# A graph layer on Trainium2: two small operands of VectorE's wide instructions moved from SBUF to PSUM

## The chip, the core and the metric

The kernel runs on one core of a Trainium2 chip. The time is the device time of one execution in microseconds (us), the median of three timed executions. Beside these there is one more execution, recorded by the profiler, from which every duration in this document comes. Five engines matter: PE (matrix products), DVE (VectorE), ACT (ScalarE), POOL (GpSimd, which here issues the gathers) and SP (which issues the plain transfers). SBUF and PSUM are the two memories on the core.

## The reference

One layer of graph attention over 12,500 nodes of 128 features and 200,000 edges, which come sorted by their target node.

```
h      = relu(layernorm(x))
score  = (h[dst] W_Q^T . h[src] W_K^T) / sqrt(128) * exp(-edge_weight)
keep   = the 16 best scores of each target node
alpha  = softmax of the kept scores, per target node
agg    = sum over kept edges of alpha * (h[src] W_msg^T)
out    = x + relu(h W_self^T + agg)
```

## The kernel before, in words

A short head computes `h` for all nodes, writes it to a table in DRAM (`h_tab`), and lays the edge data out in SBUF so that each partition holds one edge of a chunk of 128. After that the kernel is one long unrolled loop over G = 112 windows of GC = 14 chunks (1,792 edges). A window also looks at the first chunk of the next one, so up to NJ = 15 chunks take part. Nearly everything below has a width of 15 x 40 = 600 elements per partition: 15 chunks by KM = 40 slots (or WN = 40 node columns).

The rows `h[src]` come by indirect gathers on POOL (`gather`, L399): one instruction fetches 128 rows of 512 bytes by a column of 128 row numbers that lies in SBUF (`ix`, or `idx_all` for the first two windows). A window needs 14 gathers, so the whole kernel has 1,563. They go out in pairs: `let_go` (L414) copies two columns of row numbers on DVE and then issues two gathers; `hs` has seven buffers.

The steps of one window, on the other engines:

- `places` (L477, L479; DVE) makes two masks. `ow` compares the numbers 0..39 (`slots`, a 128 x 40 constant in SBUF, made once at L149) with each edge's node column (`dlw`); `po` compares the same numbers with each edge's place among the edges of its node (`pos_all`). Both are 600 elements wide.
- `q_to_edges` (L490; PE) brings the query rows to the edges; `scores` (L500; DVE) multiplies them with the gathered rows, one instruction for a chunk.
- `scores_in_slots` (L508; DVE, 600 wide), `slots_by_node` (L515; PE), `slots_out` (L520; ACT), `best` (L529 to L541; DVE), `sum_of_exps` (L546; ACT) find the 16 best scores of each node and their sum of exponentials.
- `kept_to_edges` (L558; PE) and `on_edges` (L564 to L571; DVE) carry the result back to the edges. L569 multiplies the PSUM tile `px` (named x in the trace) with `po`, 600 wide. `exps` (L575; ACT) takes exponentials.
- `weights` (L579, L580; DVE) multiplies them into `kept`, a factor for each edge, and spreads the factors over `ow` into `alz`, 600 wide.
- `sums` (L590; PE) multiplies `alz` with the gathered rows into a PSUM bank (`bank("a", 1)`, taken anew for each window, one buffer), `sums_out` (L595; ACT) reads it, and L598 to L616 finish and store the window's output.

The order on each engine is the order of the calls in the loop at L630 to L676, because scheduling is manual. One pass `i` works on several windows at once: `weights(i-3)` comes before `places(i+1)`, then `best(i-2)`, `scores(i)` in four parts, and `sums(i-3)` in two parts; `sums_out(i-3)` comes near the end. The waits between engines are put in by the compiler from the tiles that instructions touch. The trace shows that it keeps two instructions apart that touch different columns of the same PSUM bank: L598 writes columns 256 to 383 of the bank `s`, and its weight load starts at 1004.74 us in one window, after L610, which reads columns 384 to 511 of it, has ended at 1004.62; the same holds in the other windows.

A general path for other inputs (L679 on) is skipped at run time.

Of the kernel before, what the change touches and what calls it, by code (L numbers as in the profile page):

```python
# [15 lines left out]
OP = mybir.AluOpType  # L16
# [4 lines left out]
P = 128  # L21
# [10 lines left out]
NJ = GC + 1  # L32

KM = 40

WN = 40
# [22 lines left out]
def bc(ap, n):  # L59

    return ap.unsqueeze(2).to_broadcast([ap.shape[0], ap.shape[1], n])
# [7 lines left out]
def bm(ap, n):  # L69

    return ap.unsqueeze(1).to_broadcast([ap.shape[0], n, ap.shape[1]])
# [3 lines left out]
def gnn_layer(  # L75
# [27 lines left out]
    nc = tc.nc  # L103
# [26 lines left out]
    def bank(tag, bufs):  # L130
        return psum.tile([P, 512], F32, tag=tag, bufs=bufs, name=tag)
# [16 lines left out]
    slots = const.tile([P, KM], F32, name="slots")  # L148
# [12 lines left out]
    dlw = const.tile([P, G, NJ], F32, name="dlw")  # L161
# [224 lines left out]
    with tc.tile_pool(name="win", bufs=2) as win, tc.manual_schedule():  # L386
        chunks = [min(NJ, CH - GC * g) for g in range(G)]
        own = [min(GC, CH - GC * g) for g in range(G)]

        T = [{} for _ in range(G)]  # L390

        so = bank("s", 1)
        et = bank("e", 1)

        def gather(g, j0, j1, index):
            if j0 == 0:
                T[g]["hs"] = rows_pool.tile([P, GC, D], F32, name="hs", bufs=7)
            for j in range(j0, j1):
                nc.gpsimd.indirect_dma_start(  # L399
                    out=T[g]["hs"][:, j, :], out_offset=None, in_=h_tab[0:N, :],  # L400
                    in_offset=bass.IndirectOffsetOnAxis(ap=index(j), axis=0))

        def rows_of(g, j):
            return T[g]["hs"][:, j, :] if j < GC else T[g + 1]["hs"][:, 0, :]

        def let_go(g, k):

            j0, j1 = 2 * k, min(2 * k + 2, own[g])
            if j0 >= j1:
                return  # L410
            if k == 0:
                T[g]["ix"] = win.tile([P, GC], I32, name="ix", bufs=4)
            ix = T[g]["ix"]
            nc.vector.tensor_copy(ix[:, j0:j1], idx_all[:, GC * g + j0:GC * g + j1])  # L414
            gather(g, j0, j1, lambda j: ix[:, j:j + 1])
# [58 lines left out]
        def places(g):  # L474
            n = chunks[g]
            T[g]["ow"] = win.tile([P, NJ, WN], F32, name="ow", bufs=6)
            nc.vector.tensor_tensor(T[g]["ow"][:, 0:n, :], bm(slots, n), bc(dlw[:, g, 0:n], WN), op=OP.is_equal)  # L477
            T[g]["po"] = win.tile([P, NJ, KM], F32, name="po", bufs=5)
            nc.vector.tensor_tensor(T[g]["po"][:, 0:n, :], bm(slots, n),  # L479
                                    bc(pos_all[:, GC * g:GC * g + n], KM), op=OP.is_equal)  # L480


# [92 lines left out]
            nc.scalar.activation(T[g]["up"][:, 0:n], T[g]["up"][:, 0:n], AF.Exp)  # L575

        def weights(g):
            n, kept = chunks[g], T[g]["kept"]
            nc.vector.tensor_tensor(kept[:, 0:n], T[g]["up"][:, 0:n], kept[:, 0:n], op=OP.mult)  # L579
            nc.vector.tensor_tensor(alz[g % 2].rearrange("e (j w) -> e j w", w=WW + STEP)[:, 0:n, 0:WN],  # L580
                                    T[g]["ow"][:, 0:n, :], bc(kept[:, 0:n], WN), op=OP.mult)


        def sums(g, part):
            n = chunks[g]
            if part == 0:
                T[g]["pa"] = bank("a", 1)
            half = n // 2
            for j in range(half) if part == 0 else range(half, n):
                nc.tensor.matmul(T[g]["pa"][:, 0:P], lhsT=alz[g % 2][:, WW * j + PRE:WW * j + PRE + P],  # L590
                                 rhs=rows_of(g, j), start=(j == 0), stop=(j == n - 1))
# [35 lines left out]
        for g in range(min(2, G)):  # L627
            gather(g, 0, own[g], lambda j: idx_all[:, GC * g + j:GC * g + j + 1])

        for i in range(-3, G + 6):  # L630
# [5 lines left out]
            at(i - 5, output)  # L636
            at(i - 5, store)
            at(i - 3, weights)
            more(0)
            at(i - 4, sums_turned)  # L640
# [3 lines left out]
            at(i + 1, far_of)  # L644
            at(i - 1, slots_by_node)
            at(i + 1, places)
            more(1)
            at(i - 2, best)
# [8 lines left out]
            at(i + 1, q_parts)  # L657
            at(i + 2, h_turned_out)
            at(i - 3, sums, 0)
            at(i - 2, kept_to_edges)  # L660
            at(i, scores, 1)
            more(4)
            at(i, q_to_edges, 3)
            at(i - 2, one_over_sum)
            at(i - 3, sums, 1)
            at(i, scores, 2)
            at(i - 2, on_edges)
# [190 lines left out]
```

## Time and profile before

| | us |
|---|---|
| three timed executions | 2797.12, 2806.0, 2806.96; median 2806.0 |
| the profiled execution | 2125.5 |
| its span, first to last instruction | 2123.7 |
| POOL busy in the span | 1544.1 (73%) |
| DVE busy | 1488.2 (70%) |
| PE busy | 1312.0 (62%) |
| ACT busy | 626.7 (30%) |

The timed executions are 680 us longer than the profiled one. The profile doesn't show what the difference is made of. In the profiled execution the first gather starts at 79.9 us and the last at 2084.5 us, so nearly the whole span is the loop; a window takes about 17.9 us. A row of the profile names the line, the engine, the operation and the tiles (out<-in); "busy, mean ns" is the group's total and the mean of one, and what stands behind the bar is the idle time of the engine just before these instructions, with what ended it. A row of the timeline has the start in us, the duration in us and the instruction; a bracket gives the idle time before it.

### The profile page before, as it was taken

How to read it: one execution, taken by the hardware profiler on the slowest of the kernel's cores; microseconds unless marked ns; L12 is line 12 of the kernel's file. 1: busy time of each engine (PE TensorE's matmuls, PEld its weight loads, DVE VectorE, ACT ScalarE, POOL GpSimd, SP SyncE). 2: the span in 40 equal slices, each digit the busy share in tenths (PEclk: the TensorE clock that was granted, in tenths of full speed). 3: DMA queues.
4: the chain of work that ended last, by engine and by line, in shares of the span. 5: the costliest groups of instructions: out<-in, count | busy, mean ns of one | idle time of the engine just before them, and what ended most of it. 6: DMA issues, size and time to landing. Idle time of an engine off the chain costs nothing. (4 is left out here: it accounts for less than half of the span.)

```text
span 2123.7 us, 43559 instructions
## 1 busy us (share of the span) xinstructions
PE 1312.0 (62%) x14574; PEld 1210.1 (57%) x14575; DVE 1488.2 (70%) x7474; ACT 626.7 (30%) x1225; POOL 1544.1 (73%) x1585
## 2 busy tenths in 40 slices
PE   1166666666666666666666666666666666666665
PEld 1155566555555655555555656565666666565654
DVE  7667677777776777767777767677777776777764
ACT  3442222222222222222222222222222222222220
POOL 1477777777777777777777777777777777777773
PEclk9977877877777877877777777777777787877787
DMA  8453343333343343333333334334433343333420
GB/s 220 146 162 116 119 120 119 120 119 119 120 119 119 116 122 115 115 112 119 118 119 119 119 119 120 119 119 120 120 119 120 119 120 120 119 119 119 120 67 24
DMA packets 118805, 253.18 MB, mean 119 GB/s; under 512 B 33030, under 2 KB 76297, under 8 KB 118558
## 3 DMA queue, kind: packets, MB, share of 16 engines
q1 hardware_dynamic: 67336, 144.92, 19.7%
q0 software_dynamic: 50144, 102.74, 19.1%
q10 hardware_dynamic: 1094, 2.69, 0.5%
q8 instruction: 115, 1.88, 0.4%
q14 instruction: 116, 0.95, 0.1%
HBM read 236.40 MB, written 14.40 MB: 118 GB/s over the span
## 5 line engine op out<-in xcount | busy, mean ns | idle before, releaser
L399 POOL DMA_INDIRECT hs<-h_tab,ix x1535 | 1495.9, 975 | 467.8 <-issue 335.9
L500 DVE SCALAR_TENSOR_TENSOR prod<-hs,dec_all,q 128x128 f32<-128x128 f32 x1674 | 516.9, 345 | 334.3 <-DMA hs<-h_tab,ix 319.1
L490 PE MATMUL q<-q,to_e 128*128 128x128 bf16 x5022 | 464.2, 254 | 33.1 <-DVE prod L500 32.3
L598 PE MATMUL s<-ident,agn 128*128 128x128 f32 x112 | 49.3, 440 | 662.2 <-DVE kept L579 661.7
L490 PEld LDWEIGHTS <-to_e 128*128 128x128 bf16 x5022 | 410.1, 116 | 56.0 <-issue 39.8
L590 PE MATMUL a<-hs,alz 128*128 128x128 f32 x3348 | 425.8, 281 | 0.8 <-DVE alz L580 0.8
L598 PEld LDWEIGHTS s<-ident,agn 128*128 128x128 f32 x112 | 20.2, 180 | 678.4 <-issue 676.7
L590 PEld LDWEIGHTS a<-hs,alz 128*128 128x128 f32 x3348 | 404.4, 197 | 1.2 <-DVE alz L580 1.1
L515 PE MATMUL e<-ow,sl 128*41 128x40 f32 x3348 | 251.3, 265 | 8.4 <-DVE sl L508 8.4
L515 PEld LDWEIGHTS e<-ow,sl 128*41 128x41 f32 x3348 | 235.7, 184 | 23.6 <-DVE sl L508 9.2
L466 ACT ACTIVATE far<-dstb,nb 128x1920 bf16<-128x1920 int32 x112 | 212.9, 1901 | 5.1 <-DMA dstb<-in_dst_dram 5.1
L471 ACT ACTIVATE to_e<-far 128x1920 bf16<-128x1920 bf16 x112 | 201.2, 1796 | 0.1
L602 ACT COPY aggT<-s 128x128 f32<-128x128 f32 x112 | 29.8, 266 | 507.8 <-PE s L598 507.8
L529 DVE TENSOR_SCALAR ell<-slots,e 128x40 f32<-128x40 f32 x112 | 28.3, 253 | 205.3 <-PE e L515 192.6
L546 ACT ACTIVATE e<-v,km 128x16 f32<-128x16 f32 x112 | 34.4, 308 | 363.5 <-DVE km L538 363.5
L500 DVE DVE_READ_ACCUMULATOR prod<-hs,dec_all,q 128x1 f32 x1674 | 139.1, 83 | 0.2
L414 DVE COPY ix<-idx_all 128x2 int32<-128x2 int32 (+1 forms) x768 | 132.7, 173 | 0.0
L575 ACT ACTIVATE up<-up 128x15 f32<-128x15 f32 x112 | 24.1, 215 | 336.5 <-DVE up L567 336.4
L595 ACT ACTIVATE agn<-a,rden 128x128 f32<-128x128 f32 x112 | 41.2, 368 | 209.8 <-PE a L590 209.8
L508 DVE TENSOR_TENSOR sl<-po,s 128x600 f32<-128x600 f32 x112 | 87.5, 781 | 3.9
L580 DVE TENSOR_TENSOR alz<-ow,kept 128x600 f32<-128x600 f32 x112 | 87.5, 781 | 3.8
L399 POOL DMA_INDIRECT hs<-h_tab,idx_all x28 | 33.7, 1203 | 77.6 <-DMA x_end<-zpad 69.4
(150 smaller groups left out, 1562.7 us busy)
## 6 DMA issues: line engine op xcount, KB each, us to landing
dstb<-in_dst_dram SPq DMA_DIRECT2D x111, 960.0 KB
hs<-h_tab,ix POOLq DMA_INDIRECT x1535
h_r<-h_tab SPq DMA_DIRECT2D x112, 64.0 KB
x_t<-in_x_dram SPq DMA_DIRECT2D x108, 64.0 KB
out_dram<-o SPq DMA_DIRECT2D x108, 64.0 KB
xg<-in_x_dram SPq DMA_DIRECT2D x10, 560.0 KB
h_tab<-xg SPq DMA_DIRECT2D x10, 560.0 KB
dst_r<-in_dst_dram ACTq DMA_DIRECT2D x1, 803.2 KB
```

Source lines behind the costliest of these rows:

```text
L399: nc.gpsimd.indirect_dma_start(out=T[g]["hs"][:, j, :], out_offset=None, in_=h_tab[0:N, :], in_offset=bass.IndirectOffsetOnAxis(ap=index(j ...
L414: nc.vector.tensor_copy(ix[:, j0:j1], idx_all[:, GC * g + j0:GC * g + j1])
L466: nc.scalar.activation(T[g]["far"][:, 0:n], T[g]["dstb"][:, 0:n], AF.Square, bias=nb[:, g:g + 1])
L471: nc.scalar.activation(T[g]["to_e"][:, 0:n], T[g]["far"][:, 0:n], AF.Relu, bias=1.0, scale=-1.0)
L490: nc.tensor.matmul(pq[:, (j - j0) * P:(j - j0 + 1) * P], lhsT=T[g]["to_e"][:, j * P:(j + 1) * P], rhs=upper(T[g]["q"][:, k, :]), start=(k ...
L500: nc.vector.scalar_tensor_tensor(prod, rows_of(g, j), dec_all[:, c:c + 1], T[g]["pq", b][:, (j % 4) * P:(j % 4 + 1) * P], op0=OP.mult, op1 ...
L508: nc.vector.tensor_tensor(sl1[g % 2][:, 0:n, 0:KM], T[g]["po"][:, 0:n, :], bc(T[g]["s"][:, 0:n], KM), op=OP.mult)
L515: nc.tensor.matmul(et[0:KM + 1, STEP * j:STEP * j + WN], lhsT=sl1[g % 2][:, j, :], rhs=T[g]["ow"][:, j, :], start=False, stop=(j == n - 1))
L580: nc.vector.tensor_tensor(alz[g % 2].rearrange("e (j w) -> e j w", w=WW + STEP)[:, 0:n, 0:WN], T[g]["ow"][:, 0:n, :], bc(kept[:, 0:n], WN) ...
L590: nc.tensor.matmul(T[g]["pa"][:, 0:P], lhsT=alz[g % 2][:, WW * j + PRE:WW * j + PRE + P], rhs=rows_of(g, j), start=(j == 0), stop=(j == n ...
L595: nc.scalar.activation(T[g]["agn"], T[g]["pa"][:, 0:P], AF.Copy, scale=T[g]["rden"])
L598: nc.tensor.transpose(so[:, 2 * P:3 * P], T[g]["agn"], ident)
```

## The change

A PSUM bank `ab` is taken once for the loop. The slot numbers are copied into its columns 256 to 295 once; `places` reads them from there. `weights` writes its factors into the columns 384 to 398 of the same bank and reads them from there. `sums` writes its result into columns 0 to 127 of it, in place of a bank taken anew for each window. The work and its order on every engine are otherwise the same. There are no added instructions inside the loop; there is one added copy before it.

```diff
         so = bank("s", 1)
         et = bank("e", 1)
 
+        ab = bank("a", 1)
+        nc.vector.tensor_copy(ab[:, 2 * P:2 * P + KM], slots)
+
...
-            nc.vector.tensor_tensor(T[g]["ow"][:, 0:n, :], bm(slots, n), bc(dlw[:, g, 0:n], WN), op=OP.is_equal)
+            nc.vector.tensor_tensor(T[g]["ow"][:, 0:n, :], bm(ab[:, 2 * P:2 * P + KM], n), bc(dlw[:, g, 0:n], WN), op=OP.is_equal)
             T[g]["po"] = win.tile([P, NJ, KM], F32, name="po", bufs=5)
-            nc.vector.tensor_tensor(T[g]["po"][:, 0:n, :], bm(slots, n),
+            nc.vector.tensor_tensor(T[g]["po"][:, 0:n, :], bm(ab[:, 2 * P:2 * P + KM], n),
                                     bc(pos_all[:, GC * g:GC * g + n], KM), op=OP.is_equal)
...
         def weights(g):
-            n, kept = chunks[g], T[g]["kept"]
-            nc.vector.tensor_tensor(kept[:, 0:n], T[g]["up"][:, 0:n], kept[:, 0:n], op=OP.mult)
+            n, kept = chunks[g], ab[:, 3 * P:3 * P + NJ]
+            nc.vector.tensor_tensor(kept[:, 0:n], T[g]["up"][:, 0:n], T[g]["kept"][:, 0:n], op=OP.mult)
             nc.vector.tensor_tensor(alz[g % 2].rearrange("e (j w) -> e j w", w=WW + STEP)[:, 0:n, 0:WN],
                                     T[g]["ow"][:, 0:n, :], bc(kept[:, 0:n], WN), op=OP.mult)
...
         def sums(g, part):
             n = chunks[g]
-            if part == 0:
-                T[g]["pa"] = bank("a", 1)
+            T[g]["pa"] = ab
```

## The prediction

> **What bounds the kernel now.** First the page's busy times and its costliest groups:
>
> ```profile
> PE 1312.0 (62%) x14574; PEld 1210.1 (57%) x14575; DVE 1488.2 (70%) x7474; ACT 626.7 (30%) x1225; POOL 1544.1 (73%) x1585
> ...
> L399 POOL DMA_INDIRECT hs<-h_tab,ix x1535 | 1495.9, 975 | 467.8 <-issue 335.9
> L500 DVE SCALAR_TENSOR_TENSOR prod<-hs,dec_all,q 128x128 f32<-128x128 f32 x1674 | 516.9, 345 | 334.3 <-DMA hs<-h_tab,ix 319.1
> ```
>
> No engine is at 100%, so busy shares don't name the bound; the idle times do. POOL's 467.8 us before 1535 gathers is 0.305 us each. The view of POOL's waits (total us, times, longest us) shows that this is a constant, whatever ended it:
>
> ```profile
> POOL hs L399 <- issue: 343.8, 1128, 0.3
> ...
> POOL hs L399 <- DVE prod L500: 34.4, 113, 0.3
> POOL hs L399 <- DMA hs<-h_tab,ix: 31.1, 102, 0.3
> POOL hs L399 <- DVE ix L414: 26.8, 88, 0.3
> ```
>
> The view of line L399 gives the gathers' shortest, median and longest duration in ns:
>
> ```profile
> L399 POOL DMA_INDIRECT hs<-h_tab,ix x1535: 940/944/1550, 122.1 to 2084.5; - x192
> ```
>
> The longest wait of every kind is 0.3 us: in the loop POOL never waits for data or a buffer. (Its row numbers are copied about 30 us ahead, as the trace's L414 starts show.) A gather's median is 944 ns, so POOL's beat is 0.944 + 0.305 = 1.249 us, and 14 of them make 17.49 us against a window of 17.9 us. DVE in turn waits for gathered rows (319 us, some 2.9 us a window), so it follows POOL. The loop is bound by POOL's chain of gathers; a microsecond counts only if it shortens that chain.
>
> The chain has a defect: the mean is 975 ns where the median is 944 and the maximum 1550. 1535 x (975 - 944) = 47.6 us, 46.9 when I add up the excess gather by gather. The timeline shows where it is:
>
> ```profile
> 1004.32 0.94 POOL L399 DMA_INDIRECT hs<-h_tab,ix  x1 [0.30 <-issue]
> ...
> 1004.74 0.78 DVE L580 TENSOR_TENSOR alz<-ow,kept 128x600 f32<-128x600 f32 x1
> ...
> 1005.51 0.78 DVE L477 TENSOR_TENSOR ow<-slots,dlw 128x600 f32<-128x600 f32 x1
> 1005.56 1.54 POOL L399 DMA_INDIRECT hs<-h_tab,ix  x1 [0.30 <-issue]
> ...
> 1006.20 0.78 DVE L479 TENSOR_TENSOR po<-slots,pos_all 128x600 f32<-128x600 f32 x1
> ...
> 1007.41 0.94 POOL L399 DMA_INDIRECT hs<-h_tab,ix  x1 [0.30 <-issue]
> ...
> 1018.21 0.77 DVE L569 TENSOR_TENSOR mine<-x,po 128x600 f32<-128x600 f32 x1
> ...
> 1018.64 0.94 POOL L399 DMA_INDIRECT hs<-h_tab,ix  x1 [0.30 <-issue]
> ```
>
> The gather of 1005.56 starts under L477, both of whose inputs are in SBUF, and takes 1.54 us. The gather of 1018.64 starts under L569, which is as wide but reads one input from PSUM (x), and takes 0.94. Over the whole loop, put down to the instruction that ran when the gather started: L477 39.1 us, L479 5.5, L508 2.5, L460 0.3, all others nothing. Of the gathers that overlap L569 the mean is 943 ns.
>
> **The change part by part.**
>
> *L477 and L479 read the slot numbers from PSUM.* They keep one SBUF input, as L569 has now. By the L569 row their stalls go: 39.1 + 5.5 = 44.6 us. [...] What is late next: the freed gathers start the next beat 0.4 us a window earlier, DVE's waits for rows shrink from 2.9 us to about 2.5 a window, and POOL stays the bound.
>
> *L580 reads its factors from PSUM.* No gather loses time under it now (0 us): it ends just before a gather starts. So 0 saved here in the profiled execution; it protects from a shift in phase.
>
> *DVE's own cost.* [...] L569 with PSUM takes 773 ns, L479 without takes 775. I take 0. Either end lies in DVE's 2.5 us of waits for rows, so both add 0 to the path[...]. L579's write of 15 factors to PSUM has no near row; its SBUF form takes 163 ns. [...] I take 0, under the same cover.
>
> *The added copy* of 128x40 runs once, at the like of L539's 207 ns: 0.2 us at most, while POOL is already gathering. 0.
>
> *The added waits.* The slots, the factors and the sums now share one bank, and instructions on one bank are kept apart. PE's first L590 of a window must wait until L479 has read the bank: L590 now starts 2.9 us after L479's end (median over the windows, 1.1 at least). L579 must wait until ACT's L595 of the window before has read the bank: that ended 7.3 us earlier (median). Behind PE's wait would be queued the rest of the sums, kept_to_edges and q_to_edges, for which DVE's scores wait; behind L579, all of DVE. In the steady loop both are covered: 0 us. In the last windows, where gathers have ended and the margin of L579 falls to 0.03 us, they could show; the drain after the last gather is 38 us. I bound it by 0 and one L590 pass of about 4 us, and take 1 us. No SP transfer or POOL instruction is added or moved.
>
> Sum on the profiled execution: 2125.5 - 44.6 + 1 = 2081.9, about 44 us or 2.05% less. The medians are taken on executions of 2806 us, which the profile doesn't explain. If the extra 680 us lie outside the loop, the saving stays 44 us: 2762. If they stretch the loop, the same share gives 2806 x 0.9795 = 2748. I take the middle, 2755, with 2735 to 2770 as this case's own range.
>
> **The rivals.**
>
> *More than the profile shows* (chance 0.12). If gathers come slower in timed executions, they meet DVE in other phases, and L580 may be hit too. Three instructions of 0.78 us in 112 windows are 262 us at the very most; twice the share above gives 2691, and more is possible. For it: L580, L414, L477, L479 run in one block of 2.3 us, and a gather starts every 1.25: it is only the present phase that keeps one from starting under L580. Against: one measured phase.
>
> *The stall moves or the timed bound is another* (0.17). The gathers that no longer wait under L477 could meet L508, which keeps two SBUF inputs: a stall of 0.4 us there in each window takes all of it back. Against it: L508 follows a row's arrival, so its phase to the gathers is POOL's own, and it costs 2.5 us now. Or the timed executions are bound by something that isn't the gathers; or the PSUM operand still holds up a gather, against which L569 speaks. Each gives about 2806.
>
> *Slower: the shared bank becomes a ring* (0.11). Places, sums, sums_out and weights must then alternate on one bank. DVE has about 2.5 us a window of waits to give, and 0.4 is saved, so it decides once the new waits pass 2.9 us a window. That needs PE's sums some 10 us late against DVE, as they might be if the timed executions are slow on PE. A wait of 3.5 us gives (3.5 - 2.9) x 112 = 67 us: 2873. For it: a margin of 2.9 us on PE is small. Against: PE waits 661.7 us for DVE at L598, so it is early.
>
> *The forecast* has the remaining 0.60.
>
> **How the numbers follow.** A measurement can tell about 0.5%, 14 us, from no change. Faster: 0.60 + 0.12 = 0.72; same 0.17; slower 0.11. The range 2690 to 2812 leaves out what goes beyond twice the share (0.06) and nearly all of the slower one (0.10), below 2 in 10.
>
> **What would show it.** Right: L399's mean falls from 975 to about 946 at the same median 944; its longest is reached only in the head or under L508; L477, L479, L580 stay at 773 to 800 ns; POOL's idle stays 0.305 us each; DVE's wait for rows shrinks by some 45 us. Wrong: L399's mean stays (the PSUM operand doesn't free the gather); waits of 0.3 us give way to longer ones on POOL; L508 under long gathers; L590 waiting for L479, or L579 waiting for L595, by microseconds in every window. The profiled execution may be right and the median not: then the 680 us hold the answer.

## The result, and the profile after

| | median us | lowest to highest |
|---|---|---|
| kernel before | 2806.48 | 2797.12 to 2811.64 (4 executions) |
| kernel after | 2892.47 | 2889.23 to 2895.57 (4 executions) |

The ratio is 1.0308, with an interval of 1.029 to 1.0326: the changed kernel is 3% slower. The forecast was 2755 us, and its range ended at 2812.

One thing must be known to read this: the kernel before took 2118 to 2133 us on some chips and 2788 to 2806 us on others (medians), and in none of the later sets of runs a mixture of both. Below they are called the 2.1 ms chips and the 2.8 ms chips; each was used for one set of runs, so that it may also have been the condition of a chip at that time. The two times above are of the second kind, and the profile of before that stands ahead of the prediction (2125.5 us) is of the first. The record names no chip for these; that before and after of the table ran on the same one is assumed. The profile of after is of one execution of 2895.57 us, with a span of 2893.7. So it has to be compared with a profile of before that was taken later on another 2.8 ms chip (2787.59 us). First the busy times and groups of the page of after:

```profile
PE 1469.5 (51%) x14574; PEld 1323.0 (46%) x14575; DVE 1483.0 (51%) x7475; ACT 614.5 (21%) x1225; POOL 1526.9 (53%) x1585
...
L402 POOL DMA_INDIRECT hs<-h_tab,ix x1535 | 1480.6, 965 | 1231.1 <-issue 788.7
```

and the gathers' group of before on the other 2.8 ms chip:

```profile
L399 POOL DMA_INDIRECT hs<-h_tab,ix x1535 | 1498.9, 976 | 1106.2 <-issue 564.9
```

In the profile ahead of the prediction POOL's idle time before these gathers was 467.8 us. Here it is 1106 us before the change and 1231 after. The views of waits (total us, times, longest us) say that these are real waits. First before, on the other 2.8 ms chip:

```profile
POOL hs L399 <- issue: 573.2, 1222, 4.7
...
POOL hs L399 <- DVE prod L500: 502.2, 238, 5.3
```

and after:

```profile
ACT agn L597 <- remote: 1322.0, 105, 12.9
...
POOL hs L402 <- issue: 797.0, 1269, 4.6
...
DVE o L612 <- issue: 672.6, 103, 6.9
DVE ell L532 <- remote: 492.3, 100, 8.7
POOL hs L402 <- DVE prod L503: 437.4, 286, 6.5
...
DVE sl L511 <- DVE prod L503: 36.1, 88, 0.5
```

The longest wait of a gather is no longer 0.3 us but 4.7 to 5.3 before and 4.6 to 6.5 after. Counted gather by gather, 221 gaps of after are over 0.4 us and add 763 us beyond the constant 0.305; on the 2.8 ms chip with the kernel before it is 183 gaps and 638 us, and in the profile that I predicted from there is none. The lead of the row numbers tells the same: from the end of the copy on DVE to the start of its gather it is 31.6 us (median) in the profile that I predicted from, but 2.5 us with the kernel before on the 2.8 ms chip and 2.3 us after. So on these chips POOL's chain of gathers is not what sets the window; the gathers follow DVE's copies closely. (In the traces of the 2.8 ms chips some two thirds of the records of landed transfers are missing, 8,100 to 12,200 in place of 31,700, so the releasers "remote" and "issue" name nothing reliable there; the lengths of the waits stand.) The timeline of after shows one chain of it:

```profile
1000.76 0.78 DVE L511 TENSOR_TENSOR sl<-po,s 128x600 f32<-128x600 f32 x1 [0.41 <-DVE prod L503]
1001.08 1.28 POOL L402 DMA_INDIRECT hs<-h_tab,ix  x1 [0.30 <-DVE prod L503]
...
1007.97 0.37 ACT L597 ACTIVATE agn<-a,rden 128x128 f32<-128x128 f32 x1 [12.75 <-remote]
1008.11 0.29 DVE L612 SCALAR_TENSOR_TENSOR o<-s,x_t 128x128 f32<-128x128 f32 x1 [6.49 <-issue]
...
1009.38 0.16 DVE L417 COPY ix<-idx_all 128x2 int32<-128x2 int32 x1
1009.45 0.78 DVE L480 TENSOR_TENSOR ow<-a,dlw 128x600 f32<-128x600 f32 x1
1010.14 0.77 DVE L482 TENSOR_TENSOR po<-a,pos_all 128x600 f32<-128x600 f32 x1
1010.30 0.94 POOL L402 DMA_INDIRECT hs<-h_tab,ix  x1 [4.20 <-issue]
```

Read it from the bottom. The gather of 1010.30 has waited 4.20 us; it starts 0.76 us after DVE has copied its row numbers (L417, until 1009.54). DVE was late because L612 had waited 6.49 us for PE, and ACT's L597 had waited 12.75 us for PE's sums (L592). PE signals the chunks of these sums 1.43 us apart in this window (its semaphore events stand at 999.34, 1000.77, ..., 1005.02, 1006.48, 1007.90); on a 2.1 ms chip they stand 0.22 us apart. The weight loads of the same sums are recorded as done long before:

```profile
994.90 3.45 PEld L592 LDWEIGHTS a<-hs,alz 128*128 128x128 f32 x16
```

So loads can run ahead of the finished products, and a slow stretch of PE need not show in the loads. The gather of 1010.30 starts under L482 and takes 0.94 us: the edit does what was predicted for it. The gather of 1001.08 starts under L511, which still has two SBUF inputs, and takes 1.28.

### The profile page after: what moved, and what is told of

The parts are those of the page before. It is cut to its first block, busy times and chain, and to the rows that moved or that the text cites. A ratio compares the mean times of both kernels' runs of the same rounds, so it can differ in the third digit from the quotient of the medians.

```text
span 2893.7 us, 43560 instructions
## 1 busy us (share of the span) xinstructions
PE 1469.5 (51%) x14574; PEld 1323.0 (46%) x14575; DVE 1483.0 (51%) x7475; ACT 614.5 (21%) x1225; POOL 1526.9 (53%) x1585
## 3 DMA queue, kind: packets, MB, share of 16 engines
q10 hardware_dynamic: 1094, 2.69, 0.4%
## 5 line engine op out<-in xcount | busy, mean ns | idle before, releaser
L402 POOL DMA_INDIRECT hs<-h_tab,ix x1535 | 1480.6, 965 | 1231.1 <-issue 788.7
L493 PE MATMUL q<-q,to_e 128*128 128x128 bf16 x5022 | 503.2, 262 | 127.5 <-issue 64.6
L592 PE MATMUL a<-hs,alz 128*128 128x128 f32 x3348 | 509.4, 314 | 9.3 <-issue 8.2
L503 DVE SCALAR_TENSOR_TENSOR prod<-hs,dec_all,q 128x128 f32<-128x128 f32 x1674 | 483.4, 343 | 54.7 <-issue 18.9
L493 PEld LDWEIGHTS <-to_e 128*128 128x128 bf16 x5022 | 432.4, 119 | 161.5 <-issue 145.6
L592 PEld LDWEIGHTS a<-hs,alz 128*128 128x128 f32 x3348 | 484.2, 228 | 10.4 <-issue 8.3
L612 DVE SCALAR_TENSOR_TENSOR o<-s,x_t 128x128 f32<-128x128 f32 x112 | 32.6, 292 | 678.0 <-issue 672.6
L597 ACT ACTIVATE agn<-a,rden 128x128 f32<-128x128 f32 x112 | 41.1, 367 | 1351.5 <-remote 1322.0
L561 PE MATMUL x<-km,to_e 128*128 128x43 bf16 x1674 | 62.3, 184 | 254.7 <-DVE km L544 254.7
L561 PEld LDWEIGHTS <-to_e 128*128 128x128 bf16 x1674 | 51.3, 97 | 275.3 <-DVE km L544 272.8
L417 DVE COPY ix<-idx_all 128x2 int32<-128x2 int32 (+1 forms) x768 | 150.7, 197 | 0.0
L503 DVE DVE_READ_ACCUMULATOR prod<-hs,dec_all,q 128x1 f32 x1674 | 138.4, 83 | 0.1
L511 DVE TENSOR_TENSOR sl<-po,s 128x600 f32<-128x600 f32 x112 | 87.6, 782 | 36.9 <-DVE prod L503 36.1
L583 DVE TENSOR_TENSOR alz<-ow,a 128x600 f32<-128x600 f32 x112 | 87.0, 776 | 4.3 <-DVE a L582 0.5
```

Source lines behind the costliest of these rows:

```text
L402: nc.gpsimd.indirect_dma_start(out=T[g]["hs"][:, j, :], out_offset=None, in_=h_tab[0:N, :], in_offset=bass.IndirectOffsetOnAxis(ap=index(j ...
L493: nc.tensor.matmul(pq[:, (j - j0) * P:(j - j0 + 1) * P], lhsT=T[g]["to_e"][:, j * P:(j + 1) * P], rhs=upper(T[g]["q"][:, k, :]), start=(k ...
L503: nc.vector.scalar_tensor_tensor(prod, rows_of(g, j), dec_all[:, c:c + 1], T[g]["pq", b][:, (j % 4) * P:(j % 4 + 1) * P], op0=OP.mult, op1 ...
L511: nc.vector.tensor_tensor(sl1[g % 2][:, 0:n, 0:KM], T[g]["po"][:, 0:n, :], bc(T[g]["s"][:, 0:n], KM), op=OP.mult)
L561: nc.tensor.matmul(px[:, j, 0:KM + 3], lhsT=T[g]["to_e"][:, j * P:(j + 1) * P], rhs=upper(T[g]["km"]), start=True, stop=True)
```

## The experiments

The runs of one part below were made on one chip, and each ratio is to the kernel before on that chip. Edits that are called "part of the change" use the shared bank `ab`.

### The parts of the change, on a 2.1 ms chip

The kernel before again:

> The kernel before, unchanged, profiled once more, because its recorded execution took 2125.5 us while its timed ones took 2806, and the changed kernel's recorded execution took 2895.6 like its timed ones. If the timed executions run in another condition than the recorded one of before, this profile shows 2800 us, with PE's sums finishing about 1.4 us a chunk (as in the changed kernel) instead of 0.22, and gathers that wait for more than 0.3 us. If the recorded execution was typical, it shows 2125 us again, and the change itself made the sums slow.

Measured: 2119.0 us, ratio 1.0004 (0.9996 to 1.0012).

The bank alone: `ab` is taken once and the slots are copied into it, but all operands are still read from SBUF.

```diff
+        ab = bank("a", 1)
+        nc.vector.tensor_copy(ab[:, 2 * P:2 * P + KM], slots)
...
-            if part == 0:
-                T[g]["pa"] = bank("a", 1)
+            T[g]["pa"] = ab
```

> The bank is taken once and the slot numbers are copied there, but VectorE goes on reading both operands from SBUF. Theory ring (the bank shared between VectorE, TensorE and ScalarE adds waits): no VectorE access in the loop, so no wait: 2806 us, ratio 1.00. Theory operand (what matters is where VectorE reads from): also 1.00. A ratio of 1.02 or more would put the loss on the allocation, against both.

Measured: 2119.87 us, 0.9999 (0.9988 to 1.0011).

The bank, and the slot numbers read from PSUM (L480, L482), the factors left in SBUF:

```diff
-            nc.vector.tensor_tensor(T[g]["ow"][:, 0:n, :], bm(slots, n), bc(dlw[:, g, 0:n], WN), op=OP.is_equal)
+            nc.vector.tensor_tensor(T[g]["ow"][:, 0:n, :], bm(ab[:, 2 * P:2 * P + KM], n), bc(dlw[:, g, 0:n], WN), op=OP.is_equal)
...
-            nc.vector.tensor_tensor(T[g]["po"][:, 0:n, :], bm(slots, n),
+            nc.vector.tensor_tensor(T[g]["po"][:, 0:n, :], bm(ab[:, 2 * P:2 * P + KM], n),
```

> Only the slot numbers are read from PSUM. Theory ring: the sums must wait for places, and places for the sums of the pass before; the recorded starts leave 2 us of room, so a small part of the loss, 1.00 to 1.01; nearly all of the 3% is to be found with the factors. Theory operand (PSUM reads of VectorE hold something up, or free the gathers so that they collide elsewhere): two of the three moved reads are here, so 1.02 or more.

Measured: 2079.07 us, 0.9813 (0.9795 to 0.983).

The bank, and the factors in PSUM, the slot numbers left in SBUF:

```diff
-            n, kept = chunks[g], T[g]["kept"]
+            n, kept = chunks[g], ab[:, 3 * P:3 * P + NJ]
```

> Only the factors are in PSUM. Theory ring: the write of the factors has to wait until ScalarE has read the sums of the window before, which ends only after TensorE's sums of that window; this closes the ring, so 1.02 to 1.03, with VectorE waiting before L582 or its neighbours. Theory operand: one of three moved reads, under 1.01.

Measured: 2121.03 us, 1.001 (1.0001 to 1.0019).

All of the gain is in the slot numbers, and the sharing of a bank costs nothing that can be measured. The group of gathers of the page with the slots in PSUM, then with the factors in PSUM:

```profile
L402 POOL DMA_INDIRECT hs<-h_tab,ix x1535 | 1451.5, 946 | 467.8 <-issue 343.5
```

```profile
L402 POOL DMA_INDIRECT hs<-h_tab,ix x1535 | 1492.0, 972 | 467.8 <-issue 342.6
```

The idle time is the same 467.8 us; only the mean differs. 1,535 x 26 ns is 40 us, which is the gain of 39 us.

### The change again, on a 2.8 ms chip

> The changed kernel, unchanged. In the first job the kernel before took 2118 us, not 2806, and with the slot numbers alone in PSUM 2079. Theory condition (the jobs meet chips in two conditions, and the change is a gain of some 40 us in the one and a loss of some 86 us in the other): beside a kernel before of about 2118 us this takes 2075 to 2085, ratio 0.98; beside one of about 2806 us it takes 2892 again, ratio 1.03. Theory combination (the two halves together are slow, whatever the chip): over 2118 us, ratio 1.02 or more, although slots alone gave 0.98 and factors alone 1.00.

Measured: 2775.73 us, 0.9948 (0.9928 to 0.9969).

> Only the slot numbers in PSUM, once more, on the same chip as the changed kernel. Beside 2118 us: 2079 again (0.98). Beside 2806 us: theory ring says the ring is closed by the factors, so no loss here (0.98 to 1.00); theory phase (slow sums hold up the gathers, and any shift of the engines against each other can cost) says 1.00 to 1.03.

Measured: 2774.37 us, 0.9956 (0.9938 to 0.9973).

> The kernel before with a profile on the same chip. Beside 2806 us its profile should show the sums at some 1.4 us a chunk and gathers that wait for TensorE; beside 2118 us the profile is that of before again (0.22 us a chunk, 0.3 us between gathers).

Measured: 2787.59 us; its lines stand in this text where after is compared with before. The 3% loss, which was expected to come back on such a chip, didn't. The gathers' group of after here:

```profile
L402 POOL DMA_INDIRECT hs<-h_tab,ix x1535 | 1454.4, 947 | 1146.4 <-issue 794.1
```

Against before on this chip (976 ns, 1106.2 us) the gathers got 44.5 us shorter, and 40.2 of it came back as idle time: the freed POOL waits. Slots alone do as well as the whole change.

### The change on a 2.1 ms chip, and two probes of PE

> The changed kernel once more. Three jobs gave three answers: beside 2806 us 2892 (1.031), beside 2790 us 2776 (0.995), and beside 2118 us only its parts were run (0.981 for the slot numbers). Theory condition: beside about 2118 us it takes 2075 to 2085 (0.98); beside about 2800 us it lies at 0.99 to 1.03.

Measured: 2079.52 us, 0.9752 (0.9731 to 0.9772). The view of line L402:

```profile
L402 POOL DMA_INDIRECT hs<-h_tab,ix x1535: 940/944/1315, 119.4 to 2036.6; - x192
```

and the groups of this page:

```profile
L402 POOL DMA_INDIRECT hs<-h_tab,ix x1535 | 1450.5, 945 | 467.9 <-issue 299.6 <-DMA hs<-h_tab,ix 75.9 <-DVE ix L417 18.9
L503 DVE SCALAR_TENSOR_TENSOR prod<-hs,dec_all,q 128x128 f32<-128x128 f32 x1674 | 511.5, 344 | 290.1 <-DMA hs<-h_tab,ix 275.6 <-PE q L493 8.0 <-DMA hs<-h_tab,idx_all 2.0
...
L583 DVE TENSOR_TENSOR alz<-ow,a 128x600 f32<-128x600 f32 x112 | 87.0, 777 | 3.8
...
L480 DVE TENSOR_TENSOR ow<-a,dlw 128x600 f32<-128x600 f32 x112 | 86.6, 773 | 0.1
L572 DVE TENSOR_TENSOR mine<-x,po 128x600 f32<-128x600 f32 x112 | 86.3, 771 | 0.0
L482 DVE TENSOR_TENSOR po<-a,pos_all 128x600 f32<-128x600 f32 x112 | 86.2, 770 | 0.0
```

The mean has come down onto the median, DVE's waits for rows are 276 us (319 in the profile that I predicted from), and the instructions with a PSUM operand take what they took with two SBUF operands (before: L580 781 ns, L477 777, L479 773).

Two probes went with it, both of the kernel before. In the first, seven of the eight chunks of the second part of the sums are left out, so PE has some 3,100 instructions less:

```diff
-            for j in range(half) if part == 0 else range(half, n):
+            for j in range(half) if part == 0 else range(n - 1, n):
```

> The kernel before, with seven of the eight products of the second part of sums left out (the result is then not the reference's). Where the gathers bind (before about 2118 us): nothing, 1.00. Where TensorE's late sums bind (before about 2800 us): they end about 1.4 us apart there, so up to 7 x 1.4 = 10 us a window could go; the gathers then bind again and the time falls to some 2150 to 2400 us.

Measured: 2133.11 us, 0.9996 (0.9987 to 1.0005).

In the second, 15 products of one column are added in every window, some 3,400 PE instructions that do hardly any work (the 1,680 products are busy for 83.9 us in all on the 2.1 ms chip, and start 40 ns apart, median):

```diff
+            for _ in range(15):
+                nc.tensor.matmul(et[0:KM + 1, 320:321], lhsT=zrow[:, 0:KM + 1], rhs=zrow[:, 0:1], start=True, stop=True)
```

> The kernel before, with 15 products of one column added to each window on TensorE, at the head of slots_by_node, into columns nobody reads. Each is some 60 ns of work, 1 us a window. Where the gathers bind: 1.00, since TensorE has 6 us a window to spare. Where TensorE binds by its work: at most 15 x 0.06 x 112 = 100 us more, 1.03. Where it is bound by a price for each instruction rather than by work (one of 0.5 us or more): over 800 us more, 1.3.

Measured: 2133.16 us, 0.9998 (0.9987 to 1.0009).

> The kernel before with its profile on the same chip, to set beside the changed kernel's: gathers 0.3 us apart and 975 ns long if about 2118 us; waits of microseconds on VectorE's index copies and late sums if about 2800 us.

Measured: 2132.77 us. Here PE is not on the path at all.

### The same probes on a 2.8 ms chip

> As r3_half_sums (seven of the eight products of the second part of sums left out; the result is then not the reference's), for a chip on which the kernel before takes some 2800 us: if the late sums of TensorE bind there, up to 10 us a window go and it takes 2150 to 2400 us; if the sums are only seen late and something else binds, it stays within 2%. Beside 2118 to 2133 us: 1.00 again.

Measured: 2786.24 us, 0.9945 (0.9935 to 0.9955).

> As r3_tiny_products (15 products of one column added to each window on TensorE), for a chip on which the kernel before takes some 2800 us: bound by TensorE's work, at most 1.03; bound by a price for each instruction, about 1.3; TensorE not the bound, 1.00. Beside 2118 to 2133 us: 1.00 again.

Measured: 2816.28 us, 1.0068 (1.0045 to 1.0091).

Here PE is on the path, but with 15 us for 3,100 or 3,400 instructions, large or tiny: not 670 us. The timeline of PE with fewer sums shows one form of the extra time:

```profile
1006.63 0.10 PEld L490 LDWEIGHTS <-to_e 128*128 128x128 bf16 x1 [1.35 <-issue]
...
1007.36 0.10 PEld L490 LDWEIGHTS <-to_e 128*128 128x128 bf16 x1 [0.64 <-issue]
...
1009.54 0.10 PEld L490 LDWEIGHTS <-to_e 128*128 128x128 bf16 x1 [1.33 <-issue]
1009.56 0.27 PE L490 MATMUL q<-q,to_e 128*128 128x128 bf16 x1 [1.19 <-issue]
1010.27 0.10 PEld L490 LDWEIGHTS <-to_e 128*128 128x128 bf16 x1 [0.63 <-issue]
1011.67 0.26 PE L490 MATMUL q<-q,to_e 128*128 128x128 bf16 x1 [1.84 <-issue]
```

Weight loads of one group, with nothing to wait for that the profile shows, come 0.7 or 1.4 us apart. The same group on a 2.1 ms chip (kernel before again):

```profile
1002.84 1.45 PEld L490 LDWEIGHTS <-to_e 128*128 128x128 bf16 x12
```

is twelve loads in 1.45 us. I counted the spaces of 0.65 to 1.5 us between successive weight loads in the loop of the kernel before: 15, together 11 us, on the 2.1 ms chip; 713, together 719 us, on the 2.8 ms chip. Most of them stand in 115 stretches, mostly of 5 to 8.5 us, 773 us in all; the execution is 667 us longer than on the 2.1 ms chip. From one stretch to the next there are mostly 9 or 10 gathers, or 18 and 28. But this count can't stand for the extra time, since loads can run ahead: the four profiles with the slot numbers in PSUM on 2.8 ms chips have only 151 to 177 such spaces and are as long. There the slow stretches fall on the sums and show in the signals: 391 to 416 pairs of successive semaphore events of PE are 1.38 to 1.48 us apart, against 143 with the kernel before on the 2.8 ms chip and 32 to 38 with it on 2.1 ms chips.

The trace excludes two causes. Of the 713 spaces, 61% begin where the clock that PE was granted is full, so a lowered clock isn't what makes them. And they are no boundary in PE's program: the DMA table has an instruction queue of 115 packets of 16 KB in either kind of chip, of 1.06 and 0.98 us each (median). It is PE's, since it has 103 with fewer sums and 128 with the tiny products. By the count of PE instructions the spaces lie about evenly over all places between two of these packets.

### Transfers, and factors alone, on a third 2.8 ms chip

> The changed kernel on one more chip. Beside about 2118 to 2133 us: 2080 (0.975 to 0.98). Beside about 2800 us: it was 0.995 on one such chip, where its gathers hardly stalled (1 us in all), and 1.031 on another, where 89 gathers stalled under L511, the wide instruction that keeps two SBUF inputs. Theory phase: one of these two again, 0.995 with few stalls or 1.03 with some 30 us of stalls under L511.

Measured: 2785.03 us, 0.9988 (0.9978 to 0.9998).

> Only the factors in PSUM. Beside about 2118 to 2133 us: 1.00, as before. Beside about 2800 us, theory ring (the write of the factors waits for the sums' reader) gives 1.02 or more even without the slot numbers; theory phase gives 0.99 to 1.01, near the kernel before, since the gathers under L480 and L482 are held up as before.

Measured: 2785.68 us, 0.9988 (0.9978 to 0.9999).

And the kernel before with the target numbers loaded once for all windows, so that 110 of 111 transfers of 960 KB are left out:

```diff
-            T[g]["dstb"] = dstb = win.tile([P, NJ * P], I32, name="dstb")
+            if not dst0:
+                dst0.append(win.tile([P, NJ * P], I32, name="dstb", bufs=1))
+                nc.sync.dma_start(dst0[0], dst[0:NJ * P].partition_broadcast(P))
+            T[g]["dstb"] = dst0[0]
```

> The kernel before, with the target numbers loaded and spread over the partitions once for all windows (the result is then not the reference's): 110 of 111 transfers of 960 KB are left out, and with them most of the 67,336 packets of their queue. Beside 2118 to 2133 us: 1.00, since the gathers bind. Beside 2800 us: if the number of packets and instructions in flight sets the pace there, some 10 to 25% less; if TensorE's own pace does, 1.00.

Measured: 2789.02 us, 1.0002 (0.9991 to 1.0012), with 736 of the long spaces. The transfers left out, 108 of 253 MB, aren't the cause of the 2.8 ms. Neither of the other two gave a loss: the loss of 3% stays with the one set of runs of the result.

### What sets off PE's long spaces, on a fourth 2.8 ms chip

One product a chunk in place of three for the query rows:

```diff
-                for k in range(3):
+                for k in range(1):
...
-                                     start=(k == 0), stop=(k == 2))
+                                     start=(k == 0), stop=(k == 0))
```

> The kernel before, in which the query rows come to the edges by one product a chunk in place of three (3,348 of 14,574 matrix products left out, so the result is not the reference's). On a chip on which the kernel before takes 2.1 ms the gathers set the time: ratio 1.000 within 0.003. On a chip on which it takes 2.8 ms: if the slow stretches of PE come from how much PE does, a quarter fewer products should take out well over a quarter of the extra 670 us, ratio 0.94 or less; if they come however little it does, at the 4.8 ns an instruction of the earlier runs, 6,696 instructions are 32 us, ratio 0.988.

Measured: 2778.19 us, 0.9914 (0.9888 to 0.9939).

Every second gather only, each chunk pair sharing one:

```diff
-            for j in range(j0, j1):
+            for j in range(j0, j1, 2):
...
-            return T[g]["hs"][:, j, :] if j < GC else T[g + 1]["hs"][:, 0, :]
+            return T[g]["hs"][:, j - j % 2, :] if j < GC else T[g + 1]["hs"][:, 0, :]
```

> The kernel before, in which only every second gather of a window is issued and its rows are used for two chunks (half the gathers left out, so the result is not the reference's). On a chip on which the kernel before takes 2.1 ms: the chain of gathers falls from 17.5 to 8.7 us a window, the next bound is VectorE with some 13.3 us of busy time and its own gaps, so 0.80 to 0.92. On a chip on which it takes 2.8 ms: if the slow stretches of PE are set off by the gathers' traffic or the gathers still carry the time, 0.90 or less; if PE's stretches carry it whatever the gathers do, 0.97 to 1.00.

Measured: 1726.87 us, 0.6158 (0.6142 to 0.6175). The page's busy times, and two of its groups:

```profile
PE 1266.1 (73%) x14574; PEld 1171.1 (68%) x14575; DVE 1445.6 (84%) x7474; ACT 617.2 (36%) x1225; POOL 811.3 (47%) x804
...
L399 POOL DMA_INDIRECT hs<-h_tab,ix x768 | 776.8, 1012 | 787.3 <-DVE prod L500 472.2
L500 DVE SCALAR_TENSOR_TENSOR prod<-hs,dec_all,q 128x128 f32<-128x128 f32 x1674 | 483.4, 343 | 13.6 <-PE q L490 8.7
```

PE has as many instructions as before, but 38 long spaces (30 us) in place of the 713 of the other 2.8 ms chip, and 22 pairs of signals 1.43 us apart in place of 143. Both signs of the slow stretches are nearly gone. A quarter fewer products had left 339 spaces (330 us), and 157 pairs of signals, and hardly moved the time; DVE stood idle as long as before (1312 us, 1303 on the other chip). So PE's slow stretches go with the gathers. Which part of a gather does it, its issue, its transfers or its signals, was not separated. With half of the gathers DVE is busy for 84% and waits little before L500 (13.6 us), so it is the likely bound. What was run on no 2.1 ms chip is this kernel, so I can't say how much of the 1727 us it would share with one.

## Why the prediction was wrong

**The cost of the stalls: right, on the chip that I read.** The change measured 2079.5 us on a 2.1 ms chip, 53 us less than before on it; 2.05% was forecast, 2.48% measured (2.28 to 2.69). The slots alone gave 1.87%. The difference lies in the same term: on that chip the kernel before has a gather mean of 979 ns, not 975, which is 6 of the missing 9 us. How many gathers start under L477 and L479 depends on the phase (70 and 39 in the profile that I read, 57 and 52 on the first chip). Under a tensor_tensor with two SBUF inputs a gather, which reads a column of row numbers from SBUF, takes up to 0.6 us more (1550 ns at most, with a median of 944, in the profile that I read). Of those that start under one with a PSUM input, some 970 in four profiles of after, none takes more than 0.02 us over the median.

**DVE's own cost: right.** L480, L482, L572 and L583 take 770 to 777 ns, the forms with two SBUF inputs (L477, L479, L580) 773 to 781: the 600-wide form with one input in PSUM and one in SBUF took no longer here. Writing the factors to PSUM costs 172 to 182 ns for 163; in the profile of after L583 waits for it 0.5 us in all.

**The added waits: right.** The bank alone is 0.9999. In the profile of after, even on the chip of the result, L592 has 9 us of idle time before all its products and L582 has 6 us before all 112, where the rival's ring needed 3.5 us in each window:

```profile
L592 PE MATMUL a<-hs,alz 128*128 128x128 f32 x3348 | 509.4, 314 | 9.3 <-issue 8.2 <-DVE alz L583 0.8
...
L582 DVE TENSOR_TENSOR a<-up,kept 128x15 f32<-128x15 f32 x112 | 20.3, 182 | 6.4
```

(The margin of L579 in the last windows, given as 0.03 us, is 0.23 us in the trace: L595 ends at 2104.04 and L579 starts at 2104.27. Nothing hangs on it.)

**The bound: wrong on the chips that were timed.** "In the loop POOL never waits for data or a buffer", and so "a microsecond counts only if it shortens that chain", was true of the profiled execution and false of the timed ones. There POOL already waited 638 us beyond its constant with the kernel before. The gathers' stalls also went (gather mean 976 to 947 ns), but 40 of 44.5 us became waits of POOL, and the time fell by 0.5% on one chip and 0.1% on another.

**The transfer to the median: this is the step that failed.** "If they stretch the loop, the same share gives 2748", and the other case, 2762, took for granted that whatever adds 680 us leaves the bound where it was. I had two executions that differed by a third and averaged over two ways of carrying a saving across, both with the same bound. The case that the timed executions are bound by something that isn't the gathers' chain stood among the rivals at about 2806, with 0.17 together with the moved stall; it is what two of the three sets of runs on 2.8 ms chips show. For the third, that of the result, this explains why the gain is missing but not the loss of 86 us.

**The 3% on top: seen, not reproduced.** In the profile of the result the rival "the stall moves to L508" is there (the line is L511 after the change). Put down to the instruction under which a gather starts, the excess of the gathers is:

| profile (2.8 ms chips) | L477/L480, L479/L482 | L580/L583 | L508/L511 |
|---|---|---|---|
| kernel before | 109 gathers, 37.4 us | 24, 8.2 us | 2, 0.7 us |
| after, another chip | none | none | 4, 0.8 us |
| after, chip of the result | none | none | 89, 30.3 us |

And it works in both directions: L511 itself starts late 88 times, each time within 0.07 us of the end of a gather that was running, 36.1 us in all; on the other chip it does so once (0.3 us). Between the spans of these two profiles of after, 2893.7 and 2778.7, the longer gathers are 26 us of the 115 and POOL's longer waits 85. A window is 24.8 us against 23.8. PE's slow signals stand in the second half of the windows in both profiles, so their place doesn't tell the two apart. That the collision under L511 causes the 85 us too, by making DVE and then PE late in each window, is my reading; no run shows it, since two other 2.8 ms chips gave 0.9948 and 0.9988 for the same kernel. The collision could also follow from a slower window instead of causing it, and if before and after of the result ran on two chips, the loss, or part of it, is a difference between these; neither was tested. Nothing supports the slower rival, the ring: its waits are not in the profile of after, and factors alone gave 0.9988 and 1.001.

**What stays open.** Why the chips differ, and how a gather makes PE late on one kind. It isn't a lowered clock, the program's blocks or the transfers of the target numbers, and the amount of PE's work moves the time by less than 1% (0.9914 to 1.0068); it goes with the number of gathers. Counted from both signs, loads and signals, the stretches stand mostly 9 or 10 gathers apart with the kernel before, 7 or 8 with the tiny products added and 12 to 16 with fewer sums, so their spacing depends on PE's instructions too; how was not shown. The recording itself isn't excluded: every later execution has a recorded span and clock, and it is on the 2.8 ms chips that records are missing. And which half of the change loses in the runs of the result: neither half was run there.

## What to carry to other kernels

When the profiled execution and the timed ones differ by much, the profile's bound is a guess for the timed ones: give "another bound" the largest share until a trace of the longer execution is read, and look first for whether the queue that you shorten ever waits there. Taking an SBUF operand of a wide VectorE instruction to PSUM freed the gathers that start under it (mean 979 to 945 ns on one chip, 976 to 947 on another), at no cost that was seen here (770 to 777 ns for 773 to 781), but the freed gathers then start at other moments relative to VectorE (103 of them under L511 in the profile of the result, 89 of these held up); count which two-SBUF instruction they will start under next. The worth of such a change isn't one number: in four comparisons it was 0.975, 0.995, 0.999 and 1.031. The slot numbers alone did as well as the whole change wherever both can be set side by side: 2079.1 and 2079.5 us on two 2.1 ms chips, 2774.4 and 2775.7 on one 2.8 ms chip.

## What the runs showed of the hardware that was not expected

- The same program takes 2.12 ms on some chips and 2.79 ms on others. DVE, ACT and POOL instructions have the same durations on both (L503 344 and 343 ns, the gathers' median 944 and 947); on the second kind PE has stretches in which it issues one weight load in 0.7 or 1.4 us, or signals one chunk of the sums in 1.43 us in place of 0.22.
- These stretches go with the gathers: half as many gathers leave 30 of 719 us of the long spaces and 22 of 143 slow pairs of signals (two chips), and the time is 0.616 of before on the same chip.
- A 600-wide instruction of VectorE with two SBUF inputs and a gather hold each other up: the gather by up to 0.6 us (1550 ns for 944), the instruction (L511) by 0.4 on average and 0.5 at most (88 times in the profile of the result).
